# Layer 0 of a two-layer graph kernel: split transposes ahead of later loads, one transpose of the src values for 13 tiles

## The chip, the cores and the metric

The kernel runs on one core of one Trainium2 chip. The metric is the device time of one execution in microseconds (us). A core has five engines that work side by side, each in its own order: TensorE (PE, matmuls; its weight loads are listed apart as PEld), VectorE (DVE), ScalarE (ACT), GpSimd (POOL) and SyncE (SP). SP computes nothing here: it issues DMA transfers, one after the other, and a transfer whose wait is not over holds up all that are behind it in SP's queue. POOL issues the DMA stores in the same way.

## The reference

There are 3327 nodes with 1024 features, and an adjacency matrix `adj` of 3327 x 3327. Cut to what matters:

```
# layer 0
h  = relu(layernorm(x))
s  = relu(quant4(h) @ quant3(weight));  s_q = quant4(s)      # small integers, scaled
x  = x + adj @ s_q                                            # scale factors left out
# layer 1 (graph attention, 8 heads of 64)
h  = relu(layernorm(x))
Wh = h @ W                                                    # 512 columns
e_src, e_dst = per head: Wh . a1, Wh . a2
att = softmax over neighbours of leaky_relu(e_src_i + e_dst_j)
x  = x + MLP(elu(att @ Wh))
```

The change lies where the two layers meet: in the stage that computes `x + adj @ s_q` for one tile of 128 rows after another and, for each finished tile, `h`, its transpose, `Wh`, `e_src` and `e_dst`.

## The kernel before

The rows are cut into T = 26 tiles of P = 128 (the last has 127). Four stages follow each other: stage 1 computes `s_q` of every tile into the SBUF tiles `s_int` (up to about 130 us of the span), **stage 2** (about 130 to 950 us) is the one described here, stage 3 is the attention (to about 1920 us) and stage 4 the MLP. Stages 1, 3 and 4 are left alone by the change.

Stage 2 takes the tiles in the order t = 0 to 25. For a tile, `mm` collects `adj @ s_q` in PSUM: 26 blocks of 128 columns of the adjacency, each split into a rounded part `hi` and a rest `lo`, each multiplied with two halves of 512 columns, so 104 matmuls per tile (line 680). The 26 blocks come in four parts of 7, 6, 7 and 6 blocks (`PARTS`), called part 0 to part 3 below. For each part, `adjacency` loads `at` through SP (line 170, three buffers), ACT rounds it to `hi` (line 174, two buffers), DVE takes `lo = at - hi` (line 178, two buffers) and compares `at` with zero into the mask `mk` (line 179), which POOL stores once per tile (line 185). Each part is fetched two parts ahead at least: the generator `columns` runs ahead of the matmuls.

When `mm` of tile t is complete, a chain starts: ACT copies it out of PSUM to `y` (line 695), DVE scales it and adds the row tile `xt` of x (lines 696, 697), which SP has loaded (line 128); the sum is stored by POOL (line 698); `normalised` takes statistics, writes `relu(x - mean)` to `y` (line 146) and gets 1/sigma from a square root on ACT and a few one-column DVE instructions (`half_inverse`, lines 133 to 136). `transposed_by_dma` then turns `y`: ACT separates the upper and lower 16 bits of each word (`yh`, line 587), one DMA transpose of 128 x 2048 two-byte elements goes through SP (`yht`, line 589), and ACT joins the halves again to `ht` (line 591). The last tile is turned by PE instead (`transposed_by_tensor`, lines 603, 604).

`heads` of tile t is placed among the matmuls of tile t+1, between its part 2 and its part 3: PE multiplies `ht` with the head weights into `whm` (line 614), ACT scales it to `wht` (line 620), DVE multiplies with a1 and a2 and sums per head into `src` and `dst` (lines 627, 628). `src`, 8 values per row, is turned by a small PE transpose into `sp` (line 633), copied to `srct` (line 635) and stored by POOL to `src_d`, the array from which stage 3 loads its rows (line 638). The rest of `heads` makes the feature arrays `fw` and `dw`, stored to `feat_d` and `dsum_d` by POOL (lines 658, 662).

The order on each engine is set by a scheduler that follows the program's dependencies, with a few instructions pinned (`keep_in_program_order`); an SBUF buffer is reused when the readers of its old contents are done.

Of the kernel before, what the change touches and what calls it, by code (L numbers as in the profile page):

```python
# [8 lines left out]
F32 = mybir.dt.float32  # L9
# [3 lines left out]
U16 = mybir.dt.uint16  # L13
I8 = mybir.dt.int8
AF = mybir.ActivationFunctionType
ALU = mybir.AluOpType
# [4 lines left out]
P = 128  # L21
N = 3327
T = (N + P - 1) // P
NP = T * P
TH = T // 2
F = 1024
KF = F // P
FC = F // 512
NH = 8
# [13 lines left out]

SUBS = [range(0, 7), range(7, 13), range(13, 20), range(20, 26)]
PARTS = SUBS
GT = 2


# [12 lines left out]
def two_layer_kernel(  # L61
# [23 lines left out]
    nc = tc.nc  # L85
# [6 lines left out]
    make_identity(nc, ident)  # L92
    ident_b = const.tile([P, P], BF16, name="ident_b")
    nc.vector.tensor_copy(ident_b, ident)
    ones = const.tile([P, P], F32, name="ones")
    nc.gpsimd.memset(ones, 1.0)
    nth = const.tile([P, P], F32, name="nth")
    nc.gpsimd.memset(nth, 1.0 / P)


    x1_d = dram.tile([NP, F], F32, name="x1_d")
# [3 lines left out]
    src_d = [dram.tile([NH, len(sub) * P], F32, name=f"src_d{i}") for i, sub in enumerate(SUBS)]  # L105
    enc_d = dram.tile([2, NP, EMB], U16, name="enc_d")

    const.tile([P, 32], F32, name="gap")
    ndst = const.tile([P, T, NH], F32, name="ndst")
    ratio = const.tile([P, T, NH], F32, name="ratio")  # L110


# [10 lines left out]
    def load_rows(dst, ap, t):  # L123

        if rows_of(t) < P:
            nc.gpsimd.memset(dst, 0.0)
        for r in row_pieces(t):
            nc.sync.dma_start(dst[r], ap[t * P + r.start : t * P + r.stop, :])

    def half_inverse(v, tag, pin=lambda ins: ins):  # L130

        s, r, q = (small.tile([P, 1], F32, tag=tag + c, name=tag + c) for c in "srq")
        pin(nc.scalar.activation(s, v, AF.Sqrt))
        pin(nc.vector.reciprocal(r, s))
        pin(nc.vector.scalar_tensor_tensor(q, v, r, s, ALU.mult, ALU.add))
        pin(nc.vector.reciprocal(r, q))
        return r

    def normalised(dst, src):

        stats = small.tile([P, FC, 6], F32, tag="stats", name="stats")
        for c in range(FC):
            nc.vector.bn_stats(stats[:, c, :], src[:, c * 512 : (c + 1) * 512])
        mv = small.tile([P, 2], F32, tag="mv", name="mv")
        nc.vector.bn_aggr(mv, stats.rearrange("p c s -> p (c s)"))
        ins = nc.vector.tensor_scalar(dst, src, mv[:, 0:1], 0.0, ALU.subtract, ALU.max)
        v = small.tile([P, 1], F32, tag="lnv", name="lnv")
        nc.vector.tensor_scalar(v, mv[:, 1:2], EPS, None, ALU.add)
        r = half_inverse(v, "ln")
        nc.vector.tensor_scalar(r, r, 2.0, None, ALU.mult)  # L150
        return ins, r

    def halves_of_words(words):

        return words.bitcast(U16).rearrange("p (n two) -> p two n", two=2)
# [6 lines left out]

    with tc.tile_pool(name="at", bufs=2, reuse_waits="tile") as atp:

        def adjacency(t, js, mk):

            nj = len(js)
            r = slice(js[0], js[0] + nj)
            at = atp.tile([P, 7, P], F32, tag="at", name="at", bufs=3)[:, :nj]
            ins = nc.sync.dma_start(at, adj_t[t][:, r, :])  # L170
            if t == 0:
                tc.keep_in_program_order(ins)
            hi = atp.tile([P, 7, P], F32R, tag="hi", name="hi")[:, :nj]
            ins = nc.scalar.copy(hi, at)  # L174
            if t == 0:
                tc.keep_in_program_order(ins)
            lo = atp.tile([P, 7, P], F32R, tag="lo", name="lo")[:, :nj]
            nc.vector.tensor_tensor(lo, at, hi.bitcast(F32), ALU.subtract)  # L178
            ins = nc.vector.tensor_scalar(mk[:, r], at, 0.0, None, ALU.is_gt)  # L179
            if t == 0:  # L180
                tc.keep_in_program_order(ins)
            if js is PARTS[-1]:
                if t == T - 1:
                    nc.vector.memset(mk[:, :, rows_of(t) :], 1)
                nc.gpsimd.dma_start(mask_d[t], mk)
            return hi, lo

        def adjacencies():
            for t in range(T):
                mk = atp.tile([P, T, P], U8, tag="mk", name="mk")  # L190
                for js in PARTS:
                    yield adjacency(t, js, mk)

        columns = adjacencies()

# [3 lines left out]
        with tc.tile_pool(name="s1", bufs=2, reuse_waits="tile") as s1, tc.tile_pool(  # L199
            name="s1_mm", bufs=3, space=PSUM, reuse_waits="tile"  # L200
        ) as mm_ps, tc.tile_pool(name="s1_tp", bufs=2, space=PSUM, reuse_waits="tile") as tp_ps:
            w_int = s1.tile([P, KF, F], BF16, name="w_int", bufs=1)
            w_stats = s1.tile([P, 2 + 4 * (KF - 2), 3], F32, name="w_stats", bufs=1)

# [367 lines left out]
        with tc.tile_pool(name="wh", bufs=1, reuse_waits="tile") as whp, tc.tile_pool(  # L572
# [10 lines left out]

            def transposed_by_dma(y):

                yh = s2.tile([P, 2, F], U16, name="yh", bufs=1)
                nc.scalar.copy(yh, halves_of_words(y))
                yht = s2.tile([P, 2 * KF, P], U16, name="yht", bufs=1)
                nc.sync.dma_start_transpose(yht, yh.rearrange("p two f -> p (two f)"))
                ht = s2.tile([P, KF, P], F32, name="ht", bufs=1)  # L590
                nc.scalar.copy(  # L591
                    halves_of_words(ht.rearrange("p k i -> p (k i)")),
                    yht.rearrange("p (two k) i -> p two (k i)", two=2),
                )
                return ht

            def transposed_by_tensor(y):
                ht = s2.tile([P, KF, P], F32, name="ht", bufs=1)
                for g in range(KF // 4):
                    tp = last_ps.tile([P, 4, P], F32, tag="last", name="tp2")  # L600
                    for q in range(4):
                        k = 4 * g + q
                        nc.tensor.transpose(tp[:, q, :], y[:, k * P : (k + 1) * P], ident)
                    nc.scalar.copy(ht[:, 4 * g : 4 * g + 4, :], tp)
                return ht

            def heads(t, ht, r):
                if t == T - 1:
# [11 lines left out]
                ins = nc.scalar.activation(wht, whm, AF.Copy, scale=r)  # L620
                if t < T - 1:
                    tc.keep_in_program_order(ins)
                src = small.tile([P, NH], F32, name="src")
                dst = small.tile([P, NH], F32, name="dst")
                for a_t, e in ((a1_t, src), (a2_t, dst)):
                    prod = s2.tile([P, EMB], F32, name="prod", bufs=1)
# [3 lines left out]
                    )  # L630
                nc.vector.tensor_scalar(ndst[:, t], dst, -1.0, None, ALU.mult)
                nc.scalar.activation(ratio[:, t], src, AF.Exp, scale=1.0 - SLOPE)
                nc.tensor.transpose(sp[:NH, :P], src, ident)
                srct = s2.tile([NH, P], F32, name="srct")
                nc.scalar.copy(srct, sp[:NH, :P])
                for sub, d in zip(SUBS, src_d):
                    if t in sub:
                        nc.gpsimd.dma_start(d[:, (t - sub[0]) * P : (t - sub[0] + 1) * P], srct)

                ft = s2.tile([P, NH, 2, HC], F32, name="ft", bufs=1)  # L640
                wh3 = wht.rearrange("p (h d) -> p h d", d=HD)
# [25 lines left out]
            before = None  # L667
            for t in range(T):
                xt = s2.tile([P, F], F32, name="xt2")
                load_rows(xt, x, t)  # L670
                mm = mm_ps.tile([P, F], F32, tag="mm", name="mm2")
                for js in PARTS:
                    hi, lo = part
                    part = next(columns, None)
                    if js is PARTS[-1] and before is not None:
                        heads(*before)
                    for q, j in enumerate(js):
                        for which in (hi, lo):
                            for c in range(FC):
                                nc.tensor.matmul(  # L680
                                    mm[:, c * 512 : (c + 1) * 512],
                                    which[:, q, :],
                                    s_int[j][:, c * 512 : (c + 1) * 512],
                                    start=(j == 0 and which is hi),
                                    stop=(j == T - 1 and which is lo),
                                )
                if t == 0:
                    for dst, ap in (
                        (whead, w_heads.rearrange("(k p) e -> p k e", p=P)),
                        (a1_t, a1.partition_broadcast(P)),  # L690
                        (a2_t, a2.partition_broadcast(P)),
                    ):
                        tc.keep_in_program_order(nc.sync.dma_start(dst, ap))
                y = s2.tile([P, F], F32, name="y", bufs=1)
                nc.scalar.activation(y, mm, AF.Copy, scale=r_asf)
                nc.vector.tensor_scalar(y, y, asf_t, sup_delta, ALU.mult, ALU.mult)
                nc.vector.tensor_tensor(xt, xt, y, ALU.add)
                nc.gpsimd.dma_start(x1_d[t * P : (t + 1) * P, :], xt)
                ln, r = normalised(y, xt)
                before = t, (transposed_by_tensor if t == T - 1 else transposed_by_dma)(y), r  # L700
            heads(*before)
    supp.close()

# [416 lines left out]
```

## Time and profile before

| | us |
|---|---|
| median of 3 runs (2239.99 to 2242.21) | 2240.26 |
| the profiled execution, its own time | 2241.67 |
| its span (first to last instruction) | 2239.9 |

The granted TensorE clock is 0.998 over the span, so times of PE instructions in different places can be compared. Some groups of the profile that belong to stage 2 (columns: line, engine, operation, out<-in, count | busy us in all, mean ns of one | idle us of the engine just before, and what ended it):

```profile
L680 PE MATMUL mm<-s_int,hi 128*128 128x512 f32 x1352 | 427.2, 397 | 0.0
L680 PE MATMUL mm<-s_int,lo 128*128 128x512 f32 x1352 | 419.1, 391 | 0.0
L614 PE MATMUL whm<-whead,ht 128*128 128x512 f32 x416 | 184.4, 596 | 7.2 <-ACT ht L591 7.0
```

Matmul records overlap, since the profile models their ends; the distance from one start to the next is what a matmul costs. Each of these 128x512 matmuls of `mm` is listed with some 394 ns, while two of them start every 0.45 us.

```profile
300.00:400.00 100.00, 99.15 (x393) 72.59 (x392) 54.11 (x90) 49.05 (x62) 11.31 (x17) 1.00 0.54 164
500.00:600.00 100.00, 97.44 (x385) 70.96 (x384) 52.12 (x86) 48.62 (x57) 10.55 (x15) 1.00 0.63 175
```

These two rows are stretches of 100 us in stage 2: after the length come the busy us of PE, PEld, DVE, ACT and POOL with their numbers of instructions, then the granted clock, the share of the DMA engines and GB/s. DVE and ACT work half of the time.

### The profile page before, as it was taken

To read this page: it belongs to the slowest core of one execution; us is meant where nothing else is said; L and a number is where in the kernel's file an instruction comes from. 1 tells how busy PE (TensorE), PEld (TensorE's weight loads), DVE (VectorE), ACT (ScalarE), POOL (GpSimd) and SP (SyncE) were. 2 spreads that over 40 slices of the span, in tenths; PEclk is the share of its full clock that TensorE was granted. 3 is DMA by queue.
4 is the path that set the end of the run, shared out by engine and by line. 5 is a ranking of instruction groups with operands and counts; after the bars stand their busy time and mean duration, and the time that the engine had idled before them with its cause. 6 is when DMAs were issued, how large, how long until landed. Compare 5 with 4: busy or idle time off the path is not lost.

```text
span 2239.9 us, 31268 instructions
## 1 busy us (share of the span) xinstructions
PE 2190.0 (98%) x12470; PEld 1747.2 (78%) x12480; DVE 1536.8 (69%) x1996; ACT 1114.9 (50%) x1685; POOL 180.4 (8%) x269
## 2 busy tenths in 40 slices
PE   5999999999999999899999999999999999999998
PEld 2477777766677777699999999999999999744444
DVE  8745555554455545588999999999999999822211
ACT  6734444444454444357566556565555655531120
POOL 2301101110111101000000000000000000000000
PEclk9999999999999999999999999999999999999999
DMA  6665566555665556934242341654242432383311
GB/s 216 161 196 158 157 182 183 170 168 146 183 181 171 162 158 189 310 128 148 83 139 88 93 131 33 225 175 151 86 148 83 138 89 77 100 208 104 113 56 56
DMA packets 241203, 321.68 MB, mean 144 GB/s; under 512 B 104021, under 2 KB 184869, under 8 KB 241057
## 3 DMA queue, kind: packets, MB, share of 16 engines
q1 hardware_dynamic: 220504, 246.50, 36.8%
q0 software_dynamic: 20544, 73.18, 10.4%
q8 instruction: 98, 1.61, 0.3%
q14 instruction: 49, 0.39, 0.1%
q10 hardware_dynamic: 8, 0.00, 0.0%
HBM read 209.25 MB, written 86.79 MB: 132 GB/s over the span
## 4 chain that ended last, share of the span: by engine, by line
PE 53%; ACT 1%; DVE 0%; DMA 0%; issue 0%; DVEq 0%
PE acc L993 27%; PE mps L786 13%; PE o L1064 8%; PE h_ps L1027 4%; ACT enct L1049 0%; PE h_ps L949 0%; DMA weights<-in_w1t 0%; ACT h L1034 0%; DVE sel L984 0%; DVE nodes L1060 0%; ACT su L830 0%; DVE su L827 0%; DVE yo L1074 0%; ACT rest L957 0%; DVEq L1117 0%
## 5 line engine op out<-in xcount | busy, mean ns | idle before, releaser
L984 DVE SCALAR_TENSOR_TENSOR sel<-srow,ndst,mask 128x896 fp32r<-128x896 f32 (+1 forms) x832 | 864.8, 1081 | 52.3 <-PE acc L993 47.2
L786 PE MATMUL mps<-dw,mf 128*128 128x260 f32 x2704 | 452.4, 283 | 0.1
L680 PE MATMUL mm<-s_int,hi 128*128 128x512 f32 x1352 | 427.2, 397 | 0.0
L680 PE MATMUL mm<-s_int,lo 128*128 128x512 f32 x1352 | 419.1, 391 | 0.0
L993 PE MATMUL acc<-f_even,sel 128*128 128x260 f32 x2704 | 399.6, 285 | 6.7 <-issue 5.0
L993 PE MATMUL acc<-f_odd,sel 128*128 128x260 f32 x2704 | 393.8, 286 | 1.0 <-ACT xs L1008 1.0
L785 ACT CAST mf<-mask 128x1664 fp32r<-128x1664 uint8 x208 | 331.4, 1594 | 113.0 <-PE mps L786 94.9
L786 PEld LDWEIGHTS mps<-dw,mf 128*128 128x128 f32 x2704 | 377.2, 188 | 0.5 <-ACT part L790 0.3
L993 PEld LDWEIGHTS acc<-f_even,sel 128*128 128x128 f32 x2704 | 356.8, 189 | 11.7 <-issue 5.9
L993 PEld LDWEIGHTS acc<-f_odd,sel 128*128 128x128 f32 x2704 | 352.5, 188 | 8.4 <-issue 3.4
L680 PEld LDWEIGHTS mm<-s_int,hi 128*128 128x128 f32 x1352 | 253.9, 188 | 63.6 <-issue 12.0
L680 PEld LDWEIGHTS mm<-s_int,lo 128*128 128x128 f32 x1352 | 252.0, 188 | 51.4
L179 DVE TENSOR_SCALAR mk<-at 128x896 uint8<-128x896 f32 (+1 forms) x104 | 62.0, 598 | 227.1 <-DMA at<-in_adj_t 226.8
L614 PE MATMUL whm<-whead,ht 128*128 128x512 f32 x416 | 184.4, 596 | 7.2 <-ACT ht L591 7.0
L1064 PE MATMUL o<-weights,h 128*128 128x512 f32 x416 | 179.9, 592 | 0.0
L1064 PEld LDWEIGHTS o<-weights,h 128*128 128x128 f32 x416 | 79.0, 190 | 99.3 <-issue 98.3
L614 PEld LDWEIGHTS whm<-whead,ht 128*128 128x128 f32 x416 | 77.6, 190 | 101.0 <-issue 87.1
L174 ACT CAST hi<-at 128x896 fp32r<-128x896 f32 x104 | 92.4, 889 | 125.6 <-PE mm L680 85.2
L790 ACT COPY part<-mps 128x260 f32<-128x260 f32 x104 | 39.3, 378 | 193.8 <-PE mps L786 193.8
L178 DVE TENSOR_TENSOR lo<-at,hi 128x896 fp32r<-128x896 f32 x104 | 106.0, 1020 | 42.8 <-ACT hi L174 42.6
L855 POOL DMA_DIRECT2D enc_d<-eh x64 | 57.5, 903 | 935.6 <-ACT eh L853 876.0
L1034 ACT ACTIVATE h<-h_ps,rest 128x512 f32<-128x512 f32 (+1 forms) x54 | 35.1, 653 | 195.0 <-PE h_ps L1027 195.0
(162 smaller groups left out, 1676.9 us busy)
## 6 DMA issues: line engine op xcount, KB each, us to landing
feat_d<-fw POOLq DMA_DIRECT2D x26, 1040.0 KB, 5.4
f_even<-feat_d SPq DMA_DIRECT2D x7, 3380.0 KB, 13.3
f_odd<-feat_d SPq DMA_DIRECT2D x7, 3380.0 KB, 13.2
at<-in_adj_t SPq DMA_DIRECT2D x52, 448.0 KB, 3.8
at<-in_adj_t SPq DMA_DIRECT2D x52, 384.0 KB, 3.2
mask<-mask_d SPq DMA_DIRECT2D x39, 416.0 KB, 6.5
dw<-dsum_d SPq DMA_DIRECT2D x16, 910.0 KB, 8.9
dsum_d<-dw POOLq DMA_DIRECT2D x26, 520.0 KB, 6.4
```

Source lines behind the costliest of these rows:

```text
L174: ins = nc.scalar.copy(hi, at)
L178: nc.vector.tensor_tensor(lo, at, hi.bitcast(F32), ALU.subtract)
L179: ins = nc.vector.tensor_scalar(mk[:, r], at, 0.0, None, ALU.is_gt)
L614: ins = nc.tensor.matmul(whm, ht[:, k, :], whead[:, k, :], start=(k == 0), stop=(k == KF - 1))
L680: nc.tensor.matmul(mm[:, c * 512 : (c + 1) * 512], which[:, q, :], s_int[j][:, c * 512 : (c + 1) * 512], start=(j == 0 and which is hi), s ...
L785: nc.scalar.copy(mf, mask[:, j : j + TH, :])
L786: nc.tensor.matmul(ps, mf[:, j % TH, :], dw[:, j, :], start=(j == 0), stop=(j == T - 1))
L855: nc.gpsimd.dma_start(enc_d[q, sub[0] * P : (sub[-1] + 1) * P, h * HD : (h + 1) * HD].rearrange("(b p) d -> p b d", p=P), eh[:, q].rearran ...
L984: nc.vector.scalar_tensor_tensor(sel[:, :nb], srow[:, :nb], ndst[:, j, h : h + 1], mask[:, :, j, :], ALU.is_gt, ALU.mult,)
L993: nc.tensor.matmul(accs[b], sel[:, b, :], f[:, j, :], start=(j == 0), stop=(j == T - 1))
L1027: nc.tensor.matmul(ps[:, :cols], wt[:, k, m * P : (m + 1) * P], xt[:, k, :cols], start=(k == 0), stop=(k == k_n - 1),)
L1064: nc.tensor.matmul(ps[:, c * 512 : (c + 1) * 512], h3[:, k, q * P : (q + 1) * P], w4[:, k, c * 512 : (c + 1) * 512], start=(k == 0), stop= ...
```

## The change

- `transposed_by_dma` splits the tile in two column halves: two `yh` copies, two DMA transposes of 128 x 1024 two-byte elements, and two joining copies, each into its half of `ht`. `yh` and `yht` get two buffers of half the size.
- The square root and the instructions after it, which give 1/sigma, are written behind the transposes and not ahead of them.
- The loads of the next `xt` and of part 0 of each later tile's adjacency are to be issued behind the last transpose (`tc.issue_after`, an order within the queue). In SP's queue before, the transpose of tile k comes behind parts 0 and 1 of tile k+2; after, it comes directly behind part 3 of tile k+1, and then `xt` of tile k+1 and the four parts of tile k+2 follow. As a result the mask comparisons of parts 0, 1 and 2 stand next to each other on DVE, between `lo` of part 3 and `lo` of part 0; that of part 3 stands directly in front of the first multiplication with a1, as before.
- On ACT the order after is: two `yh`, table load, square root, first joining copy, `hi` of part 3, second joining copy, `hi` of part 0. Before: `yh`, table load, square root, `hi` of part 3, joining copy, `hi` of part 0.
- `src` values are kept in one array `srcs` for all tiles. PE transposes them at t = 12 (13 tiles, 104 columns), t = 24 (12 tiles) and t = 25 (one tile); the 26 small stores to `src_d` are kept, 13, 12 and 1 at a time.
- `ones` and `nth` move to a pool of stage 1; `gap` grows. The constants take the same SBUF space as before.

```diff
+BATCHES = {12: 0, T - 2: 13, T - 1: T - 1}
...
-        r = half_inverse(v, "ln")
-        nc.vector.tensor_scalar(r, r, 2.0, None, ALU.mult)
-        return ins, r
+        return ins, v
...
-            ins = nc.sync.dma_start(at, adj_t[t][:, r, :])
+
+            with tc.issue_after(turned.ins) if js is PARTS[0] and turned is not None else nullcontext():
+                ins = nc.sync.dma_start(at, adj_t[t][:, r, :])
...
-                yh = s2.tile([P, 2, F], U16, name="yh", bufs=1)
-                nc.scalar.copy(yh, halves_of_words(y))
-                yht = s2.tile([P, 2 * KF, P], U16, name="yht", bufs=1)
-                nc.sync.dma_start_transpose(yht, yh.rearrange("p two f -> p (two f)"))
+
                 ht = s2.tile([P, KF, P], F32, name="ht", bufs=1)
-                nc.scalar.copy(
-                    halves_of_words(ht.rearrange("p k i -> p (k i)")),
-                    yht.rearrange("p (two k) i -> p two (k i)", two=2),
-                )
-                return ht
+                parts = []
+                for c in range(FC):
+                    yh = s2.tile([P, 2, 512], U16, name="yh", bufs=2)
+                    nc.scalar.copy(yh, halves_of_words(y[:, c * 512 : (c + 1) * 512]))
+                    yht = s2.tile([P, KF, P], U16, name="yht", bufs=2)
+                    last = nc.sync.dma_start_transpose(yht, yh.rearrange("p two f -> p (two f)"))
+                    parts.append(yht)
+                for c, yht in enumerate(parts):
+                    nc.scalar.copy(
+                        halves_of_words(
+                            ht[:, c * KF // FC : (c + 1) * KF // FC].rearrange("p k i -> p (k i)")
+                        ),
+                        yht.rearrange("p (two k) i -> p two (k i)", two=2),
+                    )
+                return ht, last
...
-                src = small.tile([P, NH], F32, name="src")
+                src = srcs[:, t]
...
-                nc.tensor.transpose(sp[:NH, :P], src, ident)
-                srct = s2.tile([NH, P], F32, name="srct")
-                nc.scalar.copy(srct, sp[:NH, :P])
-                for sub, d in zip(SUBS, src_d):
-                    if t in sub:
-                        nc.gpsimd.dma_start(d[:, (t - sub[0]) * P : (t - sub[0] + 1) * P], srct)
+                if t in BATCHES:
+                    first = BATCHES[t]
+                    n = (t + 1 - first) * NH
+                    nc.tensor.transpose(
+                        sp[:n, :P], srcs[:, first : t + 1].rearrange("p t h -> p (t h)"), ident
+                    )
+                    srct = s2.tile([P, P], F32, name="srct")
+                    nc.scalar.copy(srct[:n], sp[:n, :P])
+                    for u in range(first, t + 1):
+                        d, sub = next((d, sub) for d, sub in zip(src_d, SUBS) if u in sub)
+                        nc.gpsimd.dma_start(
+                            d[:, (u - sub[0]) * P : (u - sub[0] + 1) * P],
+                            srct[(u - first) * NH : (u - first + 1) * NH],
+                        )
...
-                load_rows(xt, x, t)
+
+                with tc.issue_after(turned.ins) if turned is not None else nullcontext():
+                    load_rows(xt, x, t)
...
-                ln, r = normalised(y, xt)
-                before = t, (transposed_by_tensor if t == T - 1 else transposed_by_dma)(y), r
+                ln, v = normalised(y, xt)
+                ht, turned = (transposed_by_tensor if t == T - 1 else transposed_by_dma)(y)
+                r = half_inverse(v, "ln")
+                nc.vector.tensor_scalar(r, r, 2.0, None, ALU.mult)
+                before = t, ht, r
```

More of the change, by code (lines that the diff above doesn't have):

```diff
@@ L94, in two_layer_kernel @@
     nc.vector.tensor_copy(ident_b, ident)
[L95 to L98, printed above, removed]
     x1_d = dram.tile([NP, F], F32, name="x1_d")
@@ L106, in two_layer_kernel @@
     enc_d = dram.tile([2, NP, EMB], U16, name="enc_d")
-    const.tile([P, 32], F32, name="gap")
+    const.tile([P, 112], F32, name="gap")
     ndst = const.tile([P, T, NH], F32, name="ndst")
+    srcs = const.tile([P, T, NH], F32, name="srcs")
     ratio = const.tile([P, T, NH], F32, name="ratio")
@@ L163, in two_layer_kernel, with adjacency @@
     with tc.tile_pool(name="at", bufs=2, reuse_waits="tile") as atp:
-        def adjacency(t, js, mk):
+        turned = None
+        def adjacency(t, js, mk, turned):
             nj = len(js)
@@ L191, in adjacencies @@
                 for js in PARTS:
-                    yield adjacency(t, js, mk)
+                    yield adjacency(t, js, mk, turned)
         columns = adjacencies()
@@ L201, in two_layer_kernel @@
         ) as mm_ps, tc.tile_pool(name="s1_tp", bufs=2, space=PSUM, reuse_waits="tile") as tp_ps:
+            ones = s1.tile([P, P], F32, name="ones", bufs=1)
+            nc.gpsimd.memset(ones, 1.0)
+            nth = s1.tile([P, P], F32, name="nth", bufs=1)
+            nc.gpsimd.memset(nth, 1.0 / P)
             w_int = s1.tile([P, KF, F], BF16, name="w_int", bufs=1)
@@ L604, in transposed_by_tensor @@
                     nc.scalar.copy(ht[:, 4 * g : 4 * g + 4, :], tp)
-                return ht
+                return ht, None
             def heads(t, ht, r):
```

## The prediction

> **What bounds the kernel now.** I read first the page's part 1, then the busy times by stretch, then PE's timeline for one tile after another.
>
> ```profile
> PE 2190.0 (98%) x12470; PEld 1747.2 (78%) x12480; DVE 1536.8 (69%) x1996; ACT 1114.9 (50%) x1685; POOL 180.4 (8%) x269
> ```
>
> PE is the bound: only what PE executes or waits for in stage 2 can give time. The busy share hides its waits, so I measure from start to start, with PE's timeline of the head products (start, length, count, and in brackets the idle time before, with its releaser):
>
> ```profile
> 170.34 7.03 PE L614 MATMUL whm<-whead,ht 128*128 128x512 f32 x16
> ...
> 293.55 7.03 PE L614 MATMUL whm<-whead,ht 128*128 128x512 f32 x16
> 324.24 7.03 PE L614 MATMUL whm<-whead,ht 128*128 128x512 f32 x16
> ...
> 544.27 7.13 PE L614 MATMUL whm<-whead,ht 128*128 128x512 f32 x16 [0.82 <-ACT ht L591]
> ...
> 917.81 7.13 PE L614 MATMUL whm<-whead,ht 128*128 128x512 f32 x16 [1.17 <-ACT ht L591]
> ```
>
> From the first to the last are 24 tiles in 747.47 us, 31.14 each. The shortest period is 324.24 - 293.55 = 30.69, in tiles whose `whm` waits for nothing; so 24 x (31.14 - 30.69) = **10.9 us** are lost at `whm`, though the page's part 5 names only 7.0 of it as idle time. It is uneven: nothing in seven or so tiles, 0.1 to 0.4 in most, 1.0 to 1.7 in seven (386.6 to 608.6, 917.8).
>
> A second, smaller loss is the `src` transpose. PE's timeline around one:
>
> ```profile
> 521.25 0.61 PE L680 MATMUL mm<-s_int,hi 128*128 128x512 f32 x2
> 521.80 0.27 PE L633 MATMUL sp<-ident,src 128*8 128x128 f32 x1
> 521.83 0.72 PE L680 MATMUL mm<-s_int,lo 128*128 128x512 f32 x2
> 522.40 0.63 PE L680 MATMUL mm<-s_int,hi 128*128 128x512 f32 x2
> 522.87 0.62 PE L680 MATMUL mm<-s_int,lo 128*128 128x512 f32 x2
> ```
>
> Two pairs beside it start 0.58 and 0.57 us apart, where neighbours have 0.46: **0.23 us** for each transpose, its wait for `src` included.
>
> **Why `whm` waits.** ACT's timeline, then SP's, of the same tile:
>
> ```profile
> 533.37 1.90 ACT L587 COPY yh<-y 128x2048 uint16<-128x2048 uint16 x1 [1.17 <-DVE y L146]
> ...
> 541.73 2.49 ACT L591 COPY ht<-yht 128x2048 uint16<-128x2048 uint16 x1 [4.20 <-DMA yht<-yh]
> ```
>
> ```profile
> 535.29 4.44 SPq L589 DMA_TRANSPOSE yht<-yh  x1
> ```
>
> `y` is ready at 533.3, `ht` at 544.2; part 2 ends on PE near 543.3 (its last pair starts at 542.83, two matmuls of 0.227). `whm` starts at 544.27, about 1 us late.
>
> **The change, part by part.** W is the start of `whm`; the next W is to follow 30.46 later (30.69 less 0.23).
>
> *Two halves.* The nearest rows for the new transposes are in the trace: stage 1 turns 128x8x128 through SP, the same shape. The tile views (min/median/max in ns, then from issue to landing):
>
> ```profile
> L589 SPq DMA_TRANSPOSE yht<-yh x25: 2229/3575/5591, 161.2 to 907.5; - x25
> ...
> DMA to landing us min/median/max: 5.1/5.5/7.7
> ```
>
> ```profile
> L305 SPq DMA_TRANSPOSE xqt<-xq x14: 1232/1237/1657, 44.9 to 117.6; - x14
> ...
> DMA to landing us min/median/max: 3.0/4.9/5.6
> ```
>
> A half lands in 3.0 to 5.6 us. I take 4.5: the stores of `feat_d`, `dsum_d` and x1 are in flight then, as row loads are in stage 1. A half `yh` takes 1.05 (line 853 copies 896 such elements in 938 ns, 768 in 831: 0.84 ns each and 0.19 fixed). A half of `ht` is the form of line 1049, 1.33. `y` ended at W+20.9 (W = 512.44); now about W+19.8: the mask comparison that stood between `xt` and the statistics has moved behind (0.5 busy, 0.5 waiting for its load at 530.48), and the `sp` transpose no longer delays part 3. Then: first `yh` W+20.8, landing W+25.3, first half of `ht` W+26.6; `hi` of part 3 0.84 more; second transpose issued 1.24 behind the first, landing by W+26.6, second half of `ht` by W+28.8. `whm` wants the first at W+30.46 and the second four steps of 0.86 later, W+33.9. Slack 3.9 and 5.1: the 10.9 us go, even at the maximum of 5.6.
>
> *A rule against splitting.* The Trainium skill (DMA: Bandwidth & Descriptors, "Anatomy of one DMA") gives each DMA some 2.0 us of fixed cost plus bytes/436e3, fitted on POOL's path. By it a half of 262 KB is an estimated 2.6 us and the whole 3.2; if two fixed costs follow each other, the second half lands 5.2 after the first issue, 2.0 later than unsplit. By the rows it lands 1.24 + 3.0 to 5.6 = 4.2 to 6.8, against 5.1 to 7.7 unsplit. The trace decides, but the forecast is the same: the rule's worst case is far inside W+33.9.
>
> *Order in SP.* The transposes now pass two `at` loads and `xt`. These, with part 2's, come in a bunch behind them, from W+23.3. `xt` is needed by DVE some 23 us later, `hi` of part 0 not before W+30.46; it lands by about W+28.5. Nothing there is late by itself; what they do together is the loop below.
>
> *Square root later; `ones`, `nth`, `gap`.* 1/sigma is needed by `wht` at the next W+7, and is there near W+24; the memsets stay early on POOL. Nothing.
>
> *`src` in batches.* 23 PE transposes go: 23 x 0.23 = 5.3 us. The two wide ones load up to 104 columns instead of 8 (weights 0.19 against 0.08): 0.2 back. 23 copies of 0.25 leave ACT, which is half idle. POOL issues 13 and 12 stores in a row: 12 x 0.53 = 6.4 us at t = 24, so `feat_d` of that tile goes out at W+16.7, not W+15.0. Its load into `f_even` (942.72 in the trace) moves by up to 1.7; PE uses that block at about 974. If that cover failed it would cost at most those 1.7. PE's gap at the seam (930.7 to 935.7) ends with DVE's first `sel`, which follows `xt` of the last tile; it stays.
>
> **Sum.** 10.9 + 5.3 - 0.2 = 16.0. The profiled execution took 2241.67, hence 2225.7; the median of the runs is 1.4 lower, hence **2224.3 us**.
>
> **The rival that must be weighed: a loop over DVE and SP.** DVE in order, the same tile:
>
> ```profile
> 545.95 0.63 DVE L179 TENSOR_SCALAR mk<-at 128x896 uint8<-128x896 f32 x1 [4.48 <-DMA at<-in_adj_t]
> 546.49 1.08 DVE L178 TENSOR_TENSOR lo<-at,hi 128x896 fp32r<-128x896 f32 x1
> 550.77 0.56 DVE L179 TENSOR_SCALAR mk<-at 128x768 uint8<-128x768 f32 x1 [3.20 <-DMA at<-in_adj_t]
> 552.16 0.69 DVE L627 TENSOR_TENSOR prod<-wht,a_t 128x512 f32<-128x512 f32 x1 [0.82 <-ACT wht L620]
> ```
>
> The last mask comparison, which waits for part 3's load, stands in front of `prod`; that load waits for the buffer that `lo` of part 0 frees; that `lo` stands behind a mask comparison of part 2, whose load waits for `lo` of part 3. In the changed kernel `hi` of part 3 stands on ACT behind the first half of `ht`. So a ring closes: `prod` to end of `ft` 4.4, `fw` on ACT 1.1, `fw`, scaling and `xt` on DVE 3.2, statistics and `y` 2.3, `yh` 1.1, **transpose**, half `ht` 1.2, `hi` to end of `lo` 1.8, **load of part 2**, comparison 0.6 and `lo` 1.1, **load of part 3**, comparison 0.5, small hops 0.2: 17.5 us and three transfers. With 4.5, 4.45 (541.50 to 545.95) and 3.2 the ring takes 29.65, less than 30.46: PE stays the bound by 0.8 us. The margin is thin, and DMA times vary.
>
> - **The ring binds somewhat** (three transfers of 13.3, mean): period 30.77, gain 24 x 0.37 = 9; **2231**. For it: slow tiles of before had transposes of 6.5 (535.29 to 541.73). Against: one half is shorter, and no load runs beside it now.
> - **Slower.** Same ring, in every tile: it beats the old 31.14 once the three transfers exceed 13.67. With 5.6 for the half (stage 1's maximum), 5.6 for part 2's load queued behind the bunch of three (a load before needed 5.6 beside a transpose, 534.42 to 540.05) and 3.3: 14.5, period 32.0, 24 x 0.85 = 20 us lost; **2260**. Against: the bunch is issued some 4 us ahead of that load.
> - **The stall stays** through something unseen between `yh` and `whm`, and only the small transposes go: 2240.26 - 5.1 = **2235**. Against: slack of 3.9.
>
> **How the numbers follow.** Forecast 0.74 (2222 to 2227; 0.27 busy per small transpose instead of 0.23 would give one us more); ring somewhat 0.16 (2227 to 2237); slower 0.06; stall stays 0.04. Within 0.2% (4.5 us) a measurement of this kernel can't be told from no change. Faster by more: 0.74 + 0.14 + 0.02 = 0.90; same 0.04; slower 0.06. The range 2220 to 2234 holds the forecast and most of the second case.
>
> **What would show it.** `whm` starts 30.4 to 30.5 apart and no wait of PE for `ht`; `sp` three times; half transposes landing under 5 us; `prod` on DVE released by ACT's `wht`. If `prod` is released by the mask comparison or its load instead, and `whm` waits again, the ring binds. Wrong too if stage 3 starts later than its shift, which would be POOL's bunch of stores.

## The result, and the profile after

| | before | after |
|---|---|---|
| median of 4 runs, us | 2240.86 (2239.99 to 2242.21) | 2225.22 (2223.88 to 2226.68) |
| ratio, 95% interval | | 0.993 (0.9913 to 0.9947) |
| span of the profiled execution, us | 2239.9 | 2222.4 |
| 24 periods of `whm` in it, us | 747.47 | 731.39 |

The changed kernel is faster by 15.6 us, 0.7%. The first view is again PE's timeline of the head products in the changed kernel (start, length, engine, line, what, count; a bracket would give the idle time before):

```profile
382.19 7.03 PE L625 MATMUL whm<-whead,ht 128*128 128x512 f32 x16
412.65 7.03 PE L625 MATMUL whm<-whead,ht 128*128 128x512 f32 x16
443.10 7.03 PE L625 MATMUL whm<-whead,ht 128*128 128x512 f32 x16
...
504.01 7.03 PE L625 MATMUL whm<-whead,ht 128*128 128x512 f32 x16
534.46 7.03 PE L625 MATMUL whm<-whead,ht 128*128 128x512 f32 x16
```

These are the tiles in which the kernel before waited most. The starts are 30.45 or 30.46 apart and no bracket stands behind them. The page's group of the same instruction and a stretch that was shown of before say the same: no idle time, and PE busy for all of the 100 us (99.15 before).

```profile
L625 PE MATMUL whm<-whead,ht 128*128 128x512 f32 x416 | 182.9, 592 | 0.0
```

```profile
300.00:400.00 100.00, 100.00 (x400) 74.83 (x399) 57.77 (x92) 49.48 (x65) 10.34 (x15) 1.00 0.53 163
```

Only two of the 24 periods are longer than 30.47: 30.76 behind the wide transpose at t = 12, and 30.66 at the last, where the first half of `ht` came 0.2 late. Stage 2 gave 16.08 us. The rest of the difference of the spans, 1.4, is the start of stage 2: the first `whm` stands at 169.02, not 170.34. Windows over 20 to 32 and 32 to 40 us, first before, then after, show why (seventh column group: the granted clock):

```profile
20.00:32.00 12.00, 6.76 (x29) 2.86 (x29) 11.39 (x33) 9.88 (x15) 7.30 (x11) 1.00 0.38 133
32.00:40.00 8.00, 6.51 (x33) 3.22 (x34) 6.94 (x15) 5.62 (x7) 2.15 (x3) 0.79 0.37 131
```

```profile
20.00:32.00 12.00, 7.17 (x25) 3.17 (x26) 11.41 (x35) 9.49 (x15) 6.92 (x11) 1.00 0.38 135
32.00:40.00 8.00, 6.76 (x42) 3.15 (x41) 7.79 (x20) 6.72 (x8) 2.55 (x4) 1.00 0.37 131
```

In stage 1 the clock was 0.79 for 8 us in the one profile and 1.00 in the other. That belongs to the execution and not to the kernel: a second profile of the changed kernel has the dip (0.91 over 20 to 40 us) and its first `whm` at 170.01. Over the 14 profiles of this case the three with a dip have their first `whm` at 169.9 on average, the eleven without at 168.4 (167.9 to 169.0). So the dip goes with a difference of this size; that it alone makes it is not shown.

Behind stage 2 nothing moved: from the last of these `whm` to the end of the span there are 1322.1 us before and 1322.0 after. The burst of POOL's stores cost nothing.

The tile view of `yht` in the changed kernel (min/median/max):

```profile
L597 SPq DMA_TRANSPOSE yht<-yh x50: 1259/2048/3716, 158.1 to 894.2; - x50
L600 ACT COPY ht<-yht x50: 1327/1354/1369, 161.3 to 900.2; 128x1024 uint16<-128x1024 uint16 x50
...
DMA to landing us min/median/max: 3.1/4.8/6.4
```

A half lands after 4.8 where 4.5 was taken, and the slowest in this view after 6.4, beyond the 5.6 that stage 1 had shown. The view leaves out a slower one: for t = 24, the last tile that is turned by DMA, SP's timeline and then ACT's show 8.6 us from the first issue to the start of the join that waited for it.

```profile
890.38 7.28 SPq L597 DMA_TRANSPOSE yht<-yh  x2
```

```profile
899.01 2.54 ACT L600 COPY ht<-yht 128x1024 uint16<-128x1024 uint16 x2 [4.56 <-DMA yht<-yh]
```

Two loads of the mask for stage 3 were issued directly ahead of these transposes, at 888.61.

DVE's timeline of the tile W = 504.01 shows the ring of the prediction at work (it is called the loop below):

```profile
512.31 0.56 DVE L179 TENSOR_SCALAR mk<-at 128x768 uint8<-128x768 f32 x1 [3.26 <-DMA at<-in_adj_t]
512.79 0.68 DVE L638 TENSOR_TENSOR prod<-wht,a_t 128x512 f32<-128x512 f32 x1
```

`wht` was done at 511.76. `prod` starts 1.03 later, directly behind the mask comparison, which waited 3.26 for part 3's load. In 7 of the 24 tiles, all between 443 and 657 us, `prod` comes 0.3 to 1.8 late in this way; in nearly all others `wht` releases it. PE shows nothing of it.

### The profile page after: what moved, and what is told of

Same layout as the page of the kernel before. It is cut to its first block, busy times and chain, and to the rows that moved or that the text cites. A ratio compares the mean times of both kernels' runs of the same rounds, so it can differ in the third digit from the quotient of the medians.

```text
span 2222.4 us, 31259 instructions
## 1 busy us (share of the span) xinstructions
PE 2180.6 (98%) x12447; PEld 1749.5 (79%) x12457; DVE 1539.3 (69%) x1996; ACT 1113.9 (50%) x1712; POOL 176.3 (8%) x269
## 4 chain that ended last, share of the span: by engine, by line
PE 54%; ACT 1%; DVE 0%; DMA 0%; issue 0%; DVEq 0%
PE acc L1017 28%; PE mps L810 14%; PE o L1088 8%; PE h_ps L1051 4%; ACT enct L1073 0%; PE h_ps L973 0%; DMA weights<-in_w1t 0%; ACT h L1058 0%; DVE sel L1008 0%; DVE nodes L1084 0%; ACT su L854 0%; DVE su L851 0%; DVE yo L1098 0%; ACT rest L981 0%; DVEq L1141 0%
## 6 DMA issues: line engine op xcount, KB each, us to landing
f_odd<-feat_d SPq DMA_DIRECT2D x7, 3380.0 KB, 12.7
```

## Experiments

Kernels that share a time of before ran on one chip beside it, five executions of each ("batches only" 18). "Periods" is the sum of the 24 periods of `whm` in the profile, "PE waits" what PE waited in them by the waits view.

| kernel | us | before, us | ratio, 95% interval | periods | PE waits |
|---|---|---|---|---|---|
| batches only | 2237.79 | 2240.34 | 0.9989 (0.9982 to 0.9996) | 743.75 | `ht` 9.1, in 10 |
| no batches | 2233.41 | 2240.34 | 0.9966 (0.9954 to 0.9979) | 740.00 | `src` 2.5, in 5 |
| whole, ordered | 2227.63 | 2240.34 | 0.9942 (0.993 to 0.9955) | 735.07 | `ht` 2.5, in 2 |
| halves, unordered | 2223.64 | 2240.34 | 0.9922 (0.9909 to 0.9936) | 731.19 | none |
| changed again | 2223.59 | 2240.77 | 0.9926 (0.9914 to 0.9939) | 732.77 | `src` 1.5, in 1 |
| second half first | 2225.80 | 2240.77 | 0.9934 (0.992 to 0.9947) | 731.97 | `ht` 0.5, in 1 |
| second first, loop cut | 2224.53 | 2240.77 | 0.9927 (0.9915 to 0.994) | 732.14 | `ht` 0.8, in 1 |
| no batches, loop cut | 2231.41 | 2240.77 | 0.9958 (0.9946 to 0.9971) | 738.70 | `src` 1.4, in 3 |
| `hi` behind both joins | 2230.70 | 2240.04 | 0.9959 (0.9947 to 0.9972) | 738.79 | `src` 4.1, `ht` 1.2 |
| joins doubled, `hi` behind | 2228.54 | 2240.04 | 0.9952 (0.994 to 0.9965) | 736.40 | `ht` 3.3, `src` 0.6 |
| joins doubled, loop cut | 2228.22 | 2240.04 | 0.9945 (0.9931 to 0.9958) | 734.81 | `ht` 2.0, in 2 |
| square root first | 2224.29 | 2240.04 | 0.993 (0.9918 to 0.9942) | 731.19 | none |

### One part at a time: batches, halves, order

Batches alone, that is the kernel before with `srcs`, `BATCHES` and the wide transposes:

> Only the src transposes of 13, 12 and 1 tiles at once; the transposes of y stay whole and behind the loads of parts 0 and 1. Sum of the prediction (5.3 off, 0.2 back): 5.1 us below before, 2235.8 beside 2240.9, and whm still waits for ht in the same seven or more tiles, its starts 30.46 apart where it does not wait. Rival: what goes away at the small transposes comes back as a longer wait at whm, since y and ht do not come earlier: within 2 us of before.

The saving is less than the sum says, 5.1: it is 2.5 us in the runs (0.9 to 4.0 by the interval) and 3.7 in the trace. PE's timeline, two tiles of it:

```profile
540.15 7.13 PE L616 MATMUL whm<-whead,ht 128*128 128x512 f32 x16 [1.60 <-ACT ht L593]
573.29 7.13 PE L616 MATMUL whm<-whead,ht 128*128 128x512 f32 x16 [2.11 <-ACT ht L593]
```

Where `whm` does not wait, the starts are 30.46 apart, as computed, but the loss at `whm` grew from 10.9 to 12.7 us. The rival is near in size and wrong in its reason. It says that `y` and `ht` do not come earlier, and they do: the removed transpose stood ahead of part 3 of the adjacency. Over the 24 tiles `yh` starts at W+20.4 in the median (20.7 before) and `ht` is complete at W+30.5 (30.75). What came back, 1.8 us of 5.5 (24 x 0.23), came in a few tiles in which the transpose landed later. The latest is the tile W = 540.15, on ACT:

```profile
561.02 1.90 ACT L589 COPY yh<-y 128x2048 uint16<-128x2048 uint16 x1 [1.09 <-DVE y L144]
...
570.76 2.47 ACT L593 COPY ht<-yht 128x2048 uint16<-128x2048 uint16 x1 [5.50 <-DMA yht<-yh]
```

Its join starts at W+30.6, where the latest of before starts at W+29.9. Whether the batches make the transposes land later, or this one trace happened to have late ones, is not shown; the 18 runs of this kernel lie between 2234.43 and 2241.89.

From here on an edit is shown against the changed kernel. The halves and the order without batches (each tile's 8 columns are transposed and stored at once):

```diff
-                if t in BATCHES:
...
+                nc.tensor.transpose(sp[:NH, :P], src, ident)
```

> The halves and the order in SP's queue, with one small src transpose per tile as before. Sum of the prediction: whm waits for nothing, its starts 30.69 apart in every tile, 10.9 us below before: 2230.0 beside 2240.9. Rival (the loop over DVE and SP nearly binds): the small transpose delays nothing on the loop, but the period is longer, so the loop has 0.23 us more room; same time. If instead the small transposes cost more than 0.23 each when nothing else stalls, the starts are over 30.8 apart and the time is above 2232.

`whm` waits for nothing, and still the gain is 7 us in the runs and 7.5 in the trace, not 10.9. DVE's timeline and then PE's in the tile W = 630.59:

```profile
638.72 0.56 DVE L179 TENSOR_SCALAR mk<-at 128x768 uint8<-128x768 f32 x1 [3.37 <-DMA at<-in_adj_t]
639.19 0.68 DVE L638 TENSOR_TENSOR prod<-wht,a_t 128x512 f32<-128x512 f32 x1
639.91 0.69 DVE L639 TENSOR_REDUCE srcs<-prod 128x8 f32<-128x512 f32 x1
```

```profile
639.28 0.61 PE L693 MATMUL mm<-s_int,hi 128*128 128x512 f32 x2
640.66 0.27 PE L644 MATMUL sp<-ident,srcs 128*8 128x128 f32 x1 [0.76 <-DVE srcs L639]
```

The late `prod` of the loop is the same as in the changed kernel, but here an instruction of PE waits for its result: the small transpose stands in PE's order among the matmuls, and PE stood still until `srcs` was there at 640.6. The waits view has five such waits, 2.5 us in all. The two parts alone save 3.7 and 7.5 us in the traces, together 16.1. The remaining 4.9 is had only by both: with the halves nothing of the batches' gain comes back at `whm` (1.8), and the batches take away the instruction through which the loop reaches PE (2.5 of waits).

The order alone and the halves alone, both with batches:

```diff
-                parts = []
-                for c in range(FC):
...
+                yh = s2.tile([P, 2, F], U16, name="yh", bufs=1)
...
+                last = nc.sync.dma_start_transpose(yht, yh.rearrange("p two f -> p (two f)"))
```

> One transpose of the whole tile, but ahead of xt and of the loads in SP's queue, and the batches. Theory A (the order alone is enough): y ends at W+19.9, yh 1.9, landing 5.5, join 2.5, so ht is ready at about W+29.8, 0.7 ahead of whm; starts 30.46 apart, 2225.2, as in the changed kernel, with a stall of some tenths only in a tile whose transpose takes over 6.2. Theory B (the halves are what brings it, since the landing of the whole is 6.2 or more in most tiles): whm waits 0.3 to 1 us in most tiles, time 2230 to 2236.

```diff
-            with tc.issue_after(turned.ins) if js is PARTS[0] and turned is not None else nullcontext():
+            with nullcontext():
...
-                with tc.issue_after(turned.ins) if turned is not None else nullcontext():
+                with nullcontext():
```

> Two half transposes, without the order in SP's queue, and the batches: part 1 of tile k+2 stands between the two halves in SP's queue. Theory A (the halves alone are enough): the first half of ht is ready some 2 us ahead of whm and the second is wanted 3.4 later; starts 30.46 apart, 2225.2. Theory B (the loads ahead of and between the transposes hold them up): the second half is issued only when part 1's load finds its buffer, ht's second half comes after W+33.9 in some tiles and the stall moves from the first to the fifth or later head product; 2228 to 2236.

The halves alone do as much as the whole change (2223.64 beside 2223.59 for the changed kernel, each on its chip): no wait of PE. The order alone gives all but some 4 us (2226.78 to 2229.13 against 2223.02 to 2223.78 on the same chip). PE's timeline names the two tiles that make 2.9 of the 3.9 us by which its periods are longer:

```profile
566.13 7.13 PE L619 MATMUL whm<-whead,ht 128*128 128x512 f32 x16 [1.21 <-ACT ht L596]
903.00 7.13 PE L619 MATMUL whm<-whead,ht 128*128 128x512 f32 x16 [1.32 <-ACT ht L596]
```

Theory A holds for the halves. The order alone lies between its theories (2225.2 and 2230 to 2236): most tiles are as A says, but two stalls are 1.2 and 1.3 us where A allowed some tenths. The way is different. Ordered, `yh` starts at W+19.56 and the whole `ht` is ready at W+29.0 in most tiles; in the two tiles of the fence its join starts at W+29.6 and W+29.4. Unordered, `yh` starts at W+20.3, but in quick tiles the first half is joined from W+25.2 to 25.6 on, and the second at W+28 to W+31, which is in time for the fifth step.

### The loop

The second half transposed first:

```diff
-                parts = []
-                for c in range(FC):
+                parts = [None] * FC
+                for c in reversed(range(FC)):
...
-                    parts.append(yht)
+                    parts[c] = yht
```

> The changed kernel with the two half transposes issued in the other order, the joins in the same order: the first join waits for the transpose that is issued second, some 2 us later than in the changed kernel. Loop theory: the first join stands on ACT in front of hi of part 3, so the loop over DVE and SP gets 2 us longer and exceeds 30.46; starts of whm 31 to 32 apart in most tiles, prod released by the mask comparison nearly everywhere, 2238 to 2262. Rival (what counts is the slack of ht at whm, 3.9 us): the first half is still 1.5 us or more ahead of whm, no wait, 2225.

2225.8: no loss, and the loop theory's numbers are far off. But the experiment was not the one intended. The scheduler also turned the joins round: the first join reads the half that is issued first, as before: it starts at W+25.45 in quick tiles, as in the changed kernel, so the loop is not longer. What it does test is the slack of the second join: the first head product now needs it. It ends at W+28.8 in most tiles, 1.7 ahead of `whm`, and only the last of the 24 waits, 0.54: there `whm` starts at 900.77, directly behind the second join.

The same with both joins behind `hi` of part 3 (`tc.issue_after`), where the join that comes first does read the half issued second:

> The kernel with the second half transposed first, but with both joins behind hi of part 3 on ACT, so that no transpose stands in the loop any more; ht comes no earlier. Loop theory: the loss of the kernel with the second half first goes, starts of whm 30.46 apart, 2225 within 2. Rival (what hurts there is ht's own lateness): as slow as that kernel or slower by the 0.8 us per tile for which the first join now waits behind hi.

2224.5 as the loop theory has it, but with nothing lost before there is nothing to regain, so this tells the theories not apart. It measures a size, though. ACT's timeline of the tile W = 290.35:

```profile
314.20 0.83 ACT L175 CAST hi<-at 128x768 fp32r<-128x768 f32 x1 [0.78 <-PE mm L709]
316.94 2.57 ACT L605 COPY ht<-yht 128x1024 uint16<-128x1024 uint16 x2 [1.91 <-DMA yht<-yh]
```

After `hi` the join waits until 316.94, W+26.6, for the half issued second. In the changed kernel the half issued first is there at W+25.45. The two land 1.2 apart, though they are issued 2.0 apart.

The kernel without batches, loop cut in the same way:

> The kernel with halves and order but a small src transpose per tile, where PE waited 0.2 to 0.8 us for src in five tiles (2.5 in the trace); here both joins stand behind hi of part 3 on ACT. Loop theory: prod is released by wht in every tile, PE waits for no src, starts of whm 30.69 apart, stage 2 some 2.5 to 3 us shorter than in that kernel: 2230. Rival (src is late because part 3's load is slow in some tiles by itself, whatever starts it): the same waits, 2233.

Between the two: 2231.41, waits for `src` in three tiles instead of five, 1.4 us instead of 2.5. The direction is the loop's, but the intervals of the two ratios overlap, and `prod` is still late by 0.36 to 0.65 in three tiles. In two of them the traces show why: the loop has a second way through the transposes, which this edit left in place. The load of part 0 stands behind them in SP's queue. SP's timeline and then DVE's for the tile W = 446.13:

```profile
436.31 5.48 SPq L599 DMA_TRANSPOSE yht<-yh  x2
```

```profile
447.13 0.63 DVE L181 TENSOR_SCALAR mk<-at 128x896 uint8<-128x896 f32 x1 [5.77 <-DMA at<-in_adj_t]
```

The transposes hold SP for 5.5 us instead of 4.0, so part 0's load is issued at W-3.6 and not W-5.0 as in quick tiles, and the comparison that waits for it starts at W+1.0 and not some 0.4 ahead of W. The last comparison is late with it. In the third tile, W = 631.10, it is part 2's load that comes late, and why stays open.

A sharper test moves `hi` of part 3 alone, behind both joins:

```diff
-            ins = nc.scalar.copy(hi, at)
+            with tc.issue_after(joined[0].ins) if js is PARTS[-1] and joined[0] is not None else nullcontext():
+                ins = nc.scalar.copy(hi, at)
...
-                    nc.scalar.copy(
+                    joined[0] = nc.scalar.copy(
```

> The changed kernel with one instruction moved on ACT: hi of part 3 behind both joins instead of between them, some 1.3 us later. Nothing of ht's own chain changes (the second join is even 0.8 us earlier). Loop theory, from the trace of the changed kernel: in quick tiles the last mask comparison ends 0.5 us ahead of prod, so the loop takes some 29.9; with 1.3 more it takes 31.2 and binds in every tile: 24 x 0.7 = 17 us lost, 2235 to 2245, whm starts 31 or more apart, prod released by the mask comparison in every tile. Rival (the loop has slack elsewhere, the loads are started earlier or later by something else): 2224.

2230.70 beside 2224.29 for the kernel with the square root first on the same chip (no wait of PE, as will be seen): some 6 us lost by 1.3 us on ACT that `ht` does not see. The loop is real. `prod` is late by more than 0.3 in 21 of 24 tiles (7 in the changed kernel), and from 412 to 535 the lateness adds up tile by tile: 1.2, 2.5, 3.4, 3.7, 4.2. At t = 12 it meets the wide transpose. PE's timeline:

```profile
543.94 0.63 PE L703 MATMUL mm<-s_int,hi 128*128 128x512 f32 x2
548.62 0.32 PE L649 MATMUL sp<-ident,srcs 128*104 128x128 f32 x1 [4.05 <-DVE srcs L641]
548.70 0.91 PE L703 MATMUL mm<-s_int,lo 128*128 128x512 f32 x2
549.40 1.05 PE L703 MATMUL mm<-s_int,hi 128*128 128x512 f32 x2
```

Of the 7.4 us by which the periods grew, 6.15 are this one period (535.12 to 571.72, 36.60 instead of 30.45).

The price of 17 was wrong because the loop has more room than was read from the trace. That the comparison ends some 0.6 ahead of `prod` is right for most quick tiles of the changed kernel (0.2 to 1.1). But a late `prod` does not make `yh` late at once. DVE's timelines, first of the changed kernel (W = 199.47), then of this one (W = 198.87, `prod` 0.60 late):

```profile
212.45 0.96 DVE L178 TENSOR_TENSOR lo<-at,hi 128x768 fp32r<-128x768 f32 x1 [0.75 <-ACT hi L174]
```

```profile
211.85 0.96 DVE L180 TENSOR_TENSOR lo<-at,hi 128x768 fp32r<-128x768 f32 x1 [0.19 <-ACT hi L176]
```

Behind `ft` DVE waits for a `hi` of ACT, and a late `prod` first eats up this wait. In this kernel `yh` starts at W+19.56 with `prod` 0.60 late, at W+20.14 with 1.21 and at W+21.38 with 2.46: it follows only what exceeds 0.63. So a typical quick tile has an estimated 1.2 us of room (0.6 and 0.63), and the 1.3 just use it up. The loop binds in the tiles whose transposes are slow.

> As before, but each join is done twice, ahead of hi of part 3: hi of part 3 is 4.0 us later than in the changed kernel, ht's first half complete at W+29.5 and the second at W+30.9 (wanted at W+30.46 and W+33.9). Loop theory: 29.9 + 4.0 = 33.9 per tile, 2295 to 2315. Rival (only ht's slack counts): 2224, or up to 2228 with a stall in the few tiles whose transposes land a microsecond later.

> Each join done twice, but hi of part 3 ahead of them on ACT. ht is as late as in the kernel with doubled joins and hi behind, or 0.8 us later (first half W+30.2, second W+31.6). Loop theory: no transpose stands in the loop, 2224 to 2230, with a stall at whm only where the transposes land late. Rival (ht's lateness is what costs): as slow as that kernel, or slower.

The first should have been the slowest of all, and is at 2228.54. DVE's timeline around W = 290.07 shows that the loop was cut elsewhere, by the scheduler:

```profile
289.60 0.63 DVE L181 TENSOR_SCALAR mk<-at 128x896 uint8<-128x896 f32 x1 [6.07 <-DMA at<-in_adj_t]
290.81 0.96 DVE L180 TENSOR_TENSOR lo<-at,hi 128x768 fp32r<-128x768 f32 x1 [0.58 <-ACT hi L176]
291.68 0.55 DVE L181 TENSOR_SCALAR mk<-at 128x768 uint8<-128x768 f32 x1
292.15 1.08 DVE L180 TENSOR_TENSOR lo<-at,hi 128x896 fp32r<-128x896 f32 x1
295.04 0.63 DVE L181 TENSOR_SCALAR mk<-at 128x896 uint8<-128x896 f32 x1 [1.80 <-DMA at<-in_adj_t]
296.85 0.56 DVE L181 TENSOR_SCALAR mk<-at 128x768 uint8<-128x768 f32 x1 [1.19 <-DMA at<-in_adj_t]
```

`lo` of part 0 (292.15) now stands ahead of the mask comparison of part 2 (295.04), so part 3's load no longer waits for part 2's. The last comparison waits 1.2 for it instead of 3.2, and `prod` is late in 10 tiles by at most 1.5, though `hi` of part 3 comes 3.6 us later. So neither kernel is the clean pair that was wanted. Both lose some 4 us, at `whm` above all, for the doubled joins (1.84 and 1.86 in the last of the 24 tiles), and the second lies in its forecast of 2224 to 2230.

The last part, the place of the square root:

> The changed kernel with the square root and the one-column instructions ahead of the transposes, as in before: the table load and the square root stand between the two yh copies on ACT, so the second transpose is issued some 1.5 us later. Theory: the second half of ht is complete by W+30.3 instead of W+28.8 and wanted at W+33.9: no change, 2224. Rival (the second half is what is nearly late): a stall at the fifth head product in the slow tiles, 2226 to 2230.

2224.29 and no wait of PE: the place is worth nothing, as forecast.

## The prediction, point by point

- **The sum, 16.0 us, and the period, 30.46.** Right: 16.08 in the profile, 15.6 in the medians, 30.45.
- **10.9 at `whm`.** Right, and the reason too: the first half of `ht` was to be complete at W+26.6 and the second at W+28.8; they were at W+26.8 and W+28.75 in quick tiles. For the second half two errors happen to cancel: it was issued 2.0 behind the first and not 1.24, and it landed some 3.8 after its issue (tile W = 290.83) and not 4.5. The slack of 3.9 was really needed once: at t = 24, with 8.6 from issue to join where 4.5 was taken, the first half was 0.2 late.
- **0.23 for each small transpose.** The size is right (30.69 to 30.46), but the step "23 x 0.23 = 5.3" took it for a gain of its own. It is not: alone it is worth 2.5 us in the runs and 3.7 in the trace, and without it the halves lose 2.5 us to waits for `src`. The sum came out because both were done. The wide transpose at t = 12 cost 0.3 instead of 0.1, and in one profile PE waited 1.5 there for `src`.
- **The two halves against the rule of two fixed costs.** By the estimate with two fixed costs one after the other, the second half lands 2.0 later than the unsplit transpose. Measured in quick tiles it lands at W+26.6 against W+26.5 for the whole (the kernel with the order alone), and the first a microsecond ahead at W+25.45. The rows decided rightly: the estimates of 2.6 us for a half and 3.2 for the whole stand against 4.8 and 5.0 in the tile views.
- **The order in SP.** The forecast leaned on it for the earlier `y` (W+19.8; measured 19.6). It is true and not needed: with halves the kernel is as fast without it.
- **The ring as a rival.** The ring is there, as the kernel with `hi` behind both joins shows, and it did not bind. Its sum of 17.5 leaves out the wait of DVE behind `ft`: from the end of `ft` to `fw` it counts 1.1, the quick tile above has 1.73. It also leaves out the second way, through part 0's load. The margin was forecast at 0.8; in front of `prod` it is 0.2 to 1.1 in quick tiles, with 0.63 more behind it, and in seven tiles `prod` was late. What the prediction did not ask is who on PE would feel a loop that is late in some tiles only. After the change it is only the wide transpose at t = 12 (1.5 us in one profile) and, in the kernel with `hi` behind both joins, `whm` once `prod` is 3.4 late.
- **Square root, POOL's stores, the seam.** Nothing, as forecast; the gap of PE at the seam to stage 3 is 5.04 still.
- **Not seen: 1.4 us in stage 1**, where the clock of the profiled execution of before has a dip. The spans differ by 17.5 where stage 2 gives 16.1.

## What to carry to other kernels

Two savings that meet in one chain need not add: ask for each what it is worth if the other were missing. Here the parts alone gave 3.7 and 7.5 us in the traces, and both together 16.1. A small instruction on the bounding engine that waits for a slower engine's result can cost more than its own time, for there the slower engine's lateness enters; collecting such instructions takes away most of these places. When a loop is summed up, look for waits inside it: they are room that the sum hides. And before an experiment is read, look at each engine's order in its trace: twice here the scheduler had undone what the edit was meant to do, and once a queue kept a way open that the edit was to close.

## What the runs showed of the hardware

A wait of PE can cost more than itself when it is long. In the kernel with `hi` behind both joins PE stood for 4.05 us, and then its clock was halved. Windows of that stretch (the granted clock is the third number from the end):

```profile
548.00:550.00 2.00, 1.38 (x5) 1.15 (x6) 1.93 (x3) 0.47 (x2) 0.56 (x2) 0.76 0.55 217
550.00:552.00 2.00, 2.00 (x7) 1.52 (x6) 1.48 (x4) 0.32 (x2) 2.00 (x5) 0.50 0.04 6
552.00:554.00 2.00, 2.00 (x9) 1.64 (x8) 0.00 (x0) 0.63 (x1) 2.00 (x5) 0.89 0.06 8
```

The pairs of matmuls behind it start 0.85 apart instead of 0.45. That period grew by 6.15: 4.05 of waiting, 0.31 for the transpose, and the rest, 1.8, goes with the slow clock. After the longest shorter waits, 1.84 and 2.11 us, the clock stays at 1.00. The gap of PE at the seam to stage 3 shows the same; PE's timeline of before, then two windows behind it:

```profile
935.71 1.85 PE L993 MATMUL acc<-f_even,sel 128*128 128x260 f32 x7 [5.03 <-issue]
```

```profile
936.00:940.00 4.00, 3.52 (x15) 2.92 (x15) 4.00 (x8) 0.27 (x2) 0.00 (x0) 0.50 1.05 393
940.00:944.00 4.00, 4.00 (x26) 4.00 (x25) 4.00 (x6) 0.78 (x2) 0.00 (x0) 0.68 1.03 408
```

The gap is in every kernel here (5.01 to 5.06); what its slow clock costs was not measured. The Trainium skill (TensorE: Matmul & The Clock Gate, "Why this matters for your kernels") says to leave no idle gap above some 3 us between matmuls; the runs agree, with nothing measured between 2.11 and 4.05, and give the price of one.

What stays open is why the transposes land a microsecond or more later in most tiles between about 410 and 640 us, in every kernel that was run. The longest stalls lie there and at the last of the 24 tiles.
